# Edge sums in groups of six tiles instead of four, in a graph layer followed by a routed feed-forward layer

## The chip, the cores and the metric

The kernel runs on one core of a Trainium2 chip. A core has a matrix engine (PE, with its weight load PEld), a vector engine (DVE), a scalar engine (ACT), a general engine (POOL, GpSimd) and a queue engine (SP) that starts DMAs; POOL starts DMAs too, those with a list of row numbers among them. PE writes its products into PSUM, eight banks of 512 float32 numbers a partition; DVE and ACT read them there. The metric is the device time of one execution in microseconds, the median of several runs. All arithmetic is in float32.

## The reference, cut to what matters

```
N, E, H = 10000, 5000, 512
xn   = layernorm(x)                                  # each of the 10000 rows
msg  = relu(xn[src] + edge_attr @ W_e + b_e)         # 5000 edges x 512
aggr = segment_sum(msg, dst, N)                      # messages added into rows
h    = (1 + eps) * xn + aggr
h    = silu(batchnorm(h @ W1 + b1))                  # 512 -> 1024
x    = x + silu(batchnorm(h @ W2 + b2))              # 1024 -> 512
x    = x + ffn(layernorm(x))                         # routed, groups of 16 tokens
```

The edges are sorted by dst, and low rows are hit more often than high ones, so neighbouring edges often have the same target.

## The kernel before, in words

The work has stages: the edge sums, the first product with its statistics, the second product, and the feed-forward layer. The change touches the edge stage alone, the first 220 us or so. Line numbers are those of the kernel before.

**Tiles and groups.** The 5000 edges make 40 tiles of 128 (NTE), and the tiles make groups of EG = 4, ten groups. A DMA that adds rows into agg (in device memory) may not name a row twice, and two of them that run together may not touch the same row. So the kernel first adds up, within a group, all messages with the same target.

**Preparation.** SP fills agg with zeros (L212), in 11 DMAs, behind the loads of the edge data. POOL gathers the x rows of the first 20 tiles (L235). PE makes for each group a tile "row" that holds the group's targets along the free axis (`targets`, L245). DVE compares with it and counts, for each edge, earlier edges of its group with the same target (L256). An edge that is not the first gets a spare row behind the N real ones as its target (L261 to L264): to_i holds the row numbers. agg has AGG_ROWS = 83 x 128 rows for that.

**Messages.** For each group DVE makes the masks `same[i]` (L288): which edges of tile i have the target of which edges of tiles 0 to i. PE multiplies the edge attributes by W_e into a bank pm (L294), DVE adds the gathered row times its layer-norm scale (L295), ACT takes the relu (L296). Layer-norm statistics of the group after (`norm`, L273 to L277) come in between: DVE's statistics, ACT's square root (L275), DVE's reciprocal.

**Sums.** For tile i of a group PE adds into a bank pc the products of same[k][:, i] with the messages of tile k, for k from i to the end of the group (L304): 4 + 3 + 2 + 1 = 10 products a group. ACT copies the bank back into the tile (L306), and POOL starts the adding DMA (L307). The first sum of a group waits until all sums of the group before have landed (L311); those of one group run together, told apart by views of agg (L58). Behind the sums of a group POOL gathers the next four tiles, until all 40 are there. pm and pc have three banks each, and "row" two.

**What sets the order.** Each engine works off its own instructions in one order, which a planner writes from the program and from its own estimates; an instruction that waits holds up all that stand behind it. So instructions of other stages appear inside the edge stage: on DVE the 16 copies ctl (L492), that rearrange a small weight (the controller) of the last stage, on ACT and POOL the layer norm of the first rows of the next stage (L357 to L365). SP works in order too: after the zeros come small constants, two loads of x rows (L340), the controller (L73) and two small tables; then loads into buffers that were lent to the edge tiles: W2 (L327), x rows of the last stage (L560) and W1 (L395), each of which waits for the sums of those tiles to land.

**After the stage.** The next stage loads rows of agg (L346), which waits for all sums, adds them to the normalized rows (L376), turns them on PE (L379), and goes into a long run of products (L133).

Of the kernel before, what the change touches and what calls it, by code (L numbers as in the profile page):

```python
# [8 lines left out]
F32 = mybir.dt.float32  # L9
# [6 lines left out]
N, H, E, ED = 10000, 512, 5000, 64  # L16
# [6 lines left out]
P = 128  # L23
# [6 lines left out]
TE = P  # L30
NTE = -(-E // TE)
EP = TE * NTE
EG = 4
AGG_ROWS = 83 * P
assert AGG_ROWS > N + EG * TE
G = CH // T

# [13 lines left out]
def gnn_ffn_kernel(ctx: ExitStack, tc: tile.TileContext, a: dict, out: bass.AP):  # L51
    nc = tc.nc
    x = a["x"]


    agg = tc.dram_tile([AGG_ROWS, H], F32, name="agg")

    views = bass_types.dram_disjoint_views(agg, EG)  # L58

# [118 lines left out]
    with tc.tile_pool(name="pe1", bufs=1) as pe1, tc.tile_pool(name="pe", bufs=2) as pe, \  # L178
# [4 lines left out]
        def by_tile(name, past, dtype):  # L183
            flat = a[name][:whole * TE, :].rearrange("(t e) o -> t (e o)", e=TE)
            i = pe1.tile([NTE, TE], I32, name=name + "_i")
            nc.vector.memset(i, past)
            nc.sync.dma_start(out=i[:whole, :], in_=flat)
            nc.sync.dma_start(out=i[whole:NTE, :E - whole * TE], in_=a[name][whole * TE:E, :].rearrange("e o -> o e"))
            f = pe1.tile([NTE, TE], F32, name=name + "_r")
            nc.vector.tensor_copy(f, i)  # L190
            pt = ps_e.tile([TE, NTE], F32, name="row")
            nc.tensor.transpose(pt, f, ident[:NTE, :NTE])
            t = pe1.tile([TE, NTE], dtype, name=name + "_t")
            nc.vector.tensor_copy(t, pt)
            return t

        src_i = by_tile("src", 0, I32)
        dst_f = by_tile("dst", AGG_ROWS - 1, F32)
        eat = pe1.tile([ED + 1, EP], F32, name="eat")
# [9 lines left out]
        nc.sync.dma_start(out=eat[:ED, :E], in_=a["edge_attr_64"])  # L209
        for r0 in range(0, AGG_ROWS, 8 * P):  # L210
            j = min(8, (AGG_ROWS - r0) // P)
            nc.sync.dma_start(out=agg[r0:r0 + j * P, :].rearrange("(p j) d -> p j d", j=j),  # L212
                              in_=zero.to_broadcast([P, j, H]))


        before = pe1.tile([TE, EG, TE], F32, name="before")
        nc.gpsimd.memset(before, 1.0)
        nc.gpsimd.affine_select(out=before[:, EG - 1, :], in_=before[:, EG - 1, :], compare_op=ALU.is_gt, fill=0.0,
                                base=0, pattern=[[-1, TE]], channel_multiplier=1)
        groups = NTE // EG  # L220
        spare = pe1.tile([TE, groups, EG], F32, name="spare")
        nc.gpsimd.iota(spare, pattern=[[0, groups], [TE, EG]], base=N, channel_multiplier=1,
                       allow_small_or_imprecise_dtypes=True)
# [9 lines left out]
        def gather(t0, t1):  # L233
            for t in range(t0, t1):
                tc.keep_in_program_order(nc.gpsimd.indirect_dma_start(  # L235
                    out=xgs[t], out_offset=None, in_=x,
                    in_offset=bass.IndirectOffsetOnAxis(ap=src_i[:, t:t + 1], axis=0)))

        gather(0, NTE // 2)

        def targets(g):

            row = ps_e.tile([TE, EG, TE], F32, name="row")
            for i in range(EG):
                nc.tensor.transpose(row[:, i, :], dst_f[:, g * EG + i:g * EG + i + 1].to_broadcast([TE, TE]), ident)  # L245
            return row

# [2 lines left out]
        count = pe1.tile([TE, NTE], F32, name="count")  # L250
        for g in range(groups):
            row = targets(g)
            for i in range(EG):
                t = g * EG + i
                junk = pe.tile([TE, EG, TE], F32, name="junk", bufs=1)
                nc.vector.scalar_tensor_tensor(junk[:, :i + 1, :], row[:, :i + 1, :], dst_f[:, t:t + 1],  # L256
                                               before[:, EG - 1 - i:, :], op0=ALU.is_equal, op1=ALU.mult,
                                               accum_out=count[:, t:t + 1])
        away = pe1.tile([TE, NTE], F32, name="away")
        nc.vector.tensor_scalar(count, count, 1.0, None, op0=ALU.min)  # L260
        nc.vector.tensor_sub(away, spare.rearrange("p g i -> p (g i)"), dst_f)  # L261
        nc.vector.tensor_mul(away, away, count)
        to_i = pe1.tile([TE, NTE], I32, name="to_i")
        nc.vector.tensor_add(to_i, away, dst_f)  # L264

        def norm(g):

            st = pe.tile([TE, EG, 6], F32, name="st")
            mv = pe.tile([TE, EG, 2], F32, name="mv")
            rs = pe.tile([TE, EG, 1], F32, name="rs")  # L270
            sh = pe.tile([TE, EG, 1], F32, name="sh")
            for i in range(EG):
                tc.keep_in_program_order(nc.vector.bn_stats(out=st[:, i, :], in_=xgs[g * EG + i]))  # L273
                nc.vector.bn_aggr(out=mv[:, i, :], in_=st[:, i, :])
            nc.scalar.activation(rs, mv[:, :, 1:2], AF.Sqrt, bias=eps_t, scale=1.0)  # L275
            nc.vector.reciprocal(rs, rs)
            nc.vector.scalar_tensor_tensor(sh, mv[:, :, 0:1], -1.0, rs, op0=ALU.mult, op1=ALU.mult)  # L277
            return rs, sh

        last = []  # L280
        ln = norm(0)
        for g in range(groups):
            row = targets(g)

            same = [pe.tile([TE, i + 1, TE], F32, name=f"same{i}") for i in range(EG)]
            for i in range(EG):
                t = g * EG + i
                nc.vector.tensor_scalar(same[i], row[:, :i + 1, :], dst_f[:, t:t + 1], None, op0=ALU.is_equal)  # L288
            rs, sh = ln
            for i in range(EG):  # L290
                t = g * EG + i
                xg = xgs[t]
                pm = ps_e.tile([TE, H], F32, name="pm", bufs=3)
                nc.tensor.matmul(pm, lhsT=eat[:, t * TE:(t + 1) * TE], rhs=we, start=True, stop=True)  # L294
                tc.keep_in_program_order(nc.vector.scalar_tensor_tensor(xg, xg, rs[:, i, :], pm, op0=ALU.mult, op1=ALU.add))  # L295
                nc.scalar.activation(xg, xg, AF.Relu, bias=sh[:, i, :], scale=1.0)  # L296
            if g + 1 < groups:
                ln = norm(g + 1)
            sums = []
            for i in range(EG):  # L300
                t = g * EG + i
                pc = ps_e.tile([TE, H], F32, name="pc", bufs=3)
                for k in range(i, EG):
                    nc.tensor.matmul(pc, lhsT=same[k][:, i, :], rhs=xgs[g * EG + k], start=(k == i),  # L304
                                     stop=(k == EG - 1))
                nc.scalar.copy(xgs[t], pc)  # L306
                sums.append(tc.keep_in_program_order(nc.gpsimd.indirect_dma_start(  # L307
                    out=views[i], out_offset=bass.IndirectOffsetOnAxis(ap=to_i[:, t:t + 1], axis=0),
                    in_=xgs[t], in_offset=None, compute_op=ALU.add)))

            for done in last:  # L311
                tc.add_manual_dep(sums[0].ins, done.ins.name, mybir.DependencyInfo(
                    mybir.DependencyClass.Sync, mybir.DependencyReason.DATA), reason="sums in turn")
            last = sums
            at = NTE // 2 + g * EG
            gather(at, min(at + EG, NTE))
# [210 lines left out]
    pe, dve, act, pool = (InOrder(e) for e in (nc.tensor, nc.vector, nc.scalar, nc.gpsimd))  # L527
# [434 lines left out]
```

## Time and profile before

| what | value |
|---|---|
| median of three runs | 1968.99 us (1967.05 to 1970.73) |
| the profiled execution | 1968.09 us, span 1966.4 us |
| granted PE clock, mean over the span | 0.967 |
| first sum into agg issued | 79.47 us |
| last sum issued, end of issue | 213.86 us |
| first addition of agg rows (L376) | 222.34 us |
| POOL, one sum, issue to issue | 1.86 us |
| POOL, one gather, issue to issue | 1.25 to 1.3 us |
| DMA of a sum, issue to landing | 4.8 / 6.1 / 9.6 us (least, median, most) |
| ten products of a group (L304), at full clock | 8.75 us |

Times within the execution count from the start of the span. A row in order of time gives start, duration, engine, line, operation, output and inputs, shape, and how many were merged (x20: a float32 product of PE is recorded as two instructions), and in brackets the idle time of the engine before it with what ended it. A row of the waits gives the one that waited, what for, total us, how often, and the longest.

### The profile page before, as it was taken

The numbers are of one execution on the slowest core, as the hardware profiler recorded it, in microseconds if no ns is written. First come the engines' busy times: TensorE is split into PE (matmuls) and PEld (weight loads), VectorE is DVE, ScalarE is ACT, GpSimd is POOL, SyncE is SP. The second block draws the span as 40 slices with busy tenths as digits, with TensorE's granted clock in tenths as the row PEclk, the third lists the DMA queues.
The fourth block names the chain that finished last, engine by engine and source line by source line (L and its number), as shares of the span: only waits on it lengthen the run. The fifth ranks groups of instructions, "written<-read, shape, count | busy, mean of one in ns | idle before, by whom it ended". The sixth has DMA issues, their size and how long they took to land. (4 is left out here: it accounts for less than half of the span.)

```text
span 1966.4 us, 43924 instructions
## 1 busy us (share of the span) xinstructions
PE 1792.2 (91%) x19354; PEld 1029.4 (52%) x19354; DVE 1207.8 (61%) x1894; ACT 722.5 (37%) x973; POOL 621.5 (32%) x626
## 2 busy tenths in 40 slices
PE   5959399999999997999999999589999999999985
PEld 2424144444444443444444444367777777777763
DVE  8547276777777767434334334327787777777766
ACT  0324233333333315222222220255555555555432
POOL 4275333333233314333333331122323232323311
PEclk9979599999999998999999999699999999999998
DMA  9997444443444312333333331742232323232101
GB/s 349 301 228 143 99 169 170 162 158 151 162 162 162 140 42 84 125 147 128 143 125 126 125 126 42 237 129 88 87 112 79 120 79 120 80 119 70 45 24 57
DMA packets 95219, 256.37 MB, mean 130 GB/s; under 512 B 7845, under 2 KB 8435, under 8 KB 94452
## 3 DMA queue, kind: packets, MB, share of 16 engines
q1 hardware_dynamic: 86068, 232.58, 32.5%
q0 software_dynamic: 8960, 20.98, 5.3%
q8 instruction: 152, 2.49, 0.5%
q14 instruction: 39, 0.32, 0.0%
HBM read 143.47 MB, written 110.07 MB: 129 GB/s over the span
## 5 line engine op out<-in xcount | busy, mean ns | idle before, releaser
L133 PE MATMUL x<-h_s,w_u 128*128 128x500 f32 x640 | 289.1, 584 | 0.3 <-POOL h_s L123 0.3
L525 ACT COPY gs<-pb 128x1024 f32<-128x1024 f32 (+2 forms) x168 | 161.5, 1027 | 123.6 <-PE pb L525 112.0
L133 PEld LDWEIGHTS x<-h_s,w_u 128*128 128x128 f32 x640 | 122.4, 191 | 148.2 <-issue 142.9
L525 DVE STREAM_TRANSPOSE it<-it 128x1024 f32<-128x1024 f32 x152 | 174.9, 1209 | 0.1
L525 PE MATMUL pi<-gs,f_sb 128*64 128x64 f32 x5120 | 165.9, 225 | 3.3 <-ACT gs L525 1.7
L525 POOL TENSOR_TENSOR pv<-perm,odd_t 64x512 f32<-64x512 f32 (+1 forms) x80 | 99.8, 1248 | 206.8 <-PE pb L525 178.2
L525 PEld LDWEIGHTS pi<-gs,f_sb 128*64 128x64 f32 x5120 | 157.3, 140 | 11.0 <-issue 2.2
L525 PE MATMUL pb<-bd,xl 32*128 32x128 f32 x2504 | 144.7, 285 | 15.1 <-ACT it L525 8.8
L143 DVE SCALAR_TENSOR_TENSOR t<-w,s 128x500 f32<-128x500 f32 x60 | 40.7, 678 | 188.5 <-PE w L133 184.8
L133 PE MATMUL z<-h_s,w 128*128 128x500 f32 x320 | 148.3, 586 | 3.9 <-POOL h_s L123 3.9
L525 PE MATMUL pb<-f_sb,ib 32*32 32x256 f32 x5120 | 134.7, 385 | 14.2 <-ACT it L525 8.6
L525 DVE COPY it<-pb 128x1024 f32<-128x1024 f32 x76 | 93.1, 1225 | 88.6 <-PE pb L525 88.5
L133 PE MATMUL z<-h_s,w_u 128*128 128x500 f32 x320 | 144.0, 583 | 0.3 <-POOL h_s L123 0.3
L525 PEld LDWEIGHTS pb<-bd,xl 32*128 32x128 f32 x2504 | 129.0, 188 | 27.7 <-ACT it L525 13.6
L123 POOL TENSOR_TENSOR h_s<-hc 128x500 f32<-128x500 f32 x60 | 77.0, 1316 | 149.1 <-PE z L133 149.1
L525 ACT COPY it<-pb 128x1024 f32<-128x1024 f32 x76 | 79.0, 1039 | 112.1 <-PE pb L525 112.1
L138 ACT COPY s<-z 128x500 f32<-128x500 f32 x60 | 34.5, 575 | 220.2 <-PE z L133 156.4
L525 POOL TENSOR_SCALAR ln_rs<-ln_mv 128x4 f32<-128x4 f32 (+2 forms) x22 | 4.9, 224 | 302.5 <-DVE ln_mv L525 302.4
L525 PEld LDWEIGHTS pb<-f_sb,ib 32*32 32x32 f32 x5120 | 70.2, 103 | 57.1 <-ACT it L525 14.6
L133 PEld LDWEIGHTS z<-h_s,w_u 128*128 128x128 f32 x320 | 60.8, 190 | 73.9 <-issue 72.7
L123 POOL TENSOR_TENSOR h_s<-hb 128x1000 f32<-128x1000 f32 x30 | 69.6, 2335 | 91.5 <-PE z L133 65.3
L433 DVE BATCH_NORM_STATS2 st<-h 128x6 f32<-128x500 f32 x144 | 93.7, 671 | 1.3
(180 smaller groups left out, 3084.9 us busy)
## 6 DMA issues: line engine op xcount, KB each, us to landing
h1s<-h SPq DMA_DIRECT2D x36, 1000.0 KB
agg<-zero SPq DMA_DIRECT2D x10, 2048.0 KB
xt<-in_x_dram SPq DMA_DIRECT2D x20, 1000.0 KB
hc<-h1s SPq DMA_DIRECT2D x20, 1000.0 KB
h2s<-h SPq DMA_DIRECT2D x20, 1000.0 KB
x<-in_x_dram SPq DMA_DIRECT2D x39, 512.0 KB
out_dram<-x SPq DMA_DIRECT2D x39, 512.0 KB
yt<-h2s SPq DMA_DIRECT2D x76, 256.0 KB
```

Of the source, the lines that this page charges most:

```text
L123: eng.tensor_tensor(t[:, k0:k1], q(*x0, k0, k1), q(*x1, k0, k1), op)
L133: nc.tensor.matmul(bank, lhsT=us[n][:, k, m * P:(m + 1) * P], rhs=bs[n][k], start=start and k == 0, stop=k == kb - 1, skip_group_check=True)
L138: nc.scalar.copy(kept[n], banks[n])
L143: nc.vector.scalar_tensor_tensor(dst, banks[x0], sc, kept[x1], op0=op, op1=ALU.add)
L433: nc.vector.bn_stats(out=st1[:, 4 * r + m, 2 * i + t, :], in_=h1[:, r, t, :])
L525: return lambda *args, **kw: tc.keep_in_program_order(f(*args, **kw))
```

## The change

EG becomes 6: the 40 tiles make six groups of six and a last one of four. `tiles(g)` gives the number of tiles of a group. A group of six has 6 + 5 + 4 + 3 + 2 + 1 = 21 products pc. "row" takes a whole two banks for each of its two buffers (eight tiles wide), so pm and pc get two banks each, where they had three. AGG_ROWS grows to 85 x 128 for the spare rows of wider groups. The gathers behind a group's sums become six, until all 40 tiles are there.

```
-EG = 4
-AGG_ROWS = 83 * P
+EG = 6
+AGG_ROWS = 85 * P
...
-        groups = NTE // EG
+        groups = -(-NTE // EG)
...
+        def tiles(g):
+            return min(EG, NTE - g * EG)
...
-            row = ps_e.tile([TE, EG, TE], F32, name="row")
-            for i in range(EG):
+            row = ps_e.tile([TE, 8, TE], F32, name="row")
+            for i in range(tiles(g)):
                 nc.tensor.transpose(row[:, i, :], dst_f[:, g * EG + i:g * EG + i + 1].to_broadcast([TE, TE]), ident)
...
-            for i in range(EG):
+            for i in range(tiles(g)):
                 t = g * EG + i
                 xg = xgs[t]
-                pm = ps_e.tile([TE, H], F32, name="pm", bufs=3)
+                pm = ps_e.tile([TE, H], F32, name="pm")
...
-            for i in range(EG):
+            for i in range(tiles(g)):
                 t = g * EG + i
-                pc = ps_e.tile([TE, H], F32, name="pc", bufs=3)
-                for k in range(i, EG):
+                pc = ps_e.tile([TE, H], F32, name="pc")
+                for k in range(i, tiles(g)):
                     nc.tensor.matmul(pc, lhsT=same[k][:, i, :], rhs=xgs[g * EG + k], start=(k == i),
-                                     stop=(k == EG - 1))
+                                     stop=(k == tiles(g) - 1))
```

Without a `bufs` of its own a tile of this pool has two buffers. The other loops over a group's tiles (the counting, the statistics, the masks) change from EG to tiles(g) in the same way.

## The prediction

> **What bounds the kernel now.** I read the page first. PE is busy for 91% of the span, and of its digits (one for 49 us) the first, third and fifth are 5, 5 and 3; after them only the 26th and the last are as low. The change lies in those first five, so I asked for the waits up to 260 us, then for the instructions in order of time, engine by engine.
>
> ```profile
> PE 1792.2 (91%) x19354; PEld 1029.4 (52%) x19354; DVE 1207.8 (61%) x1894; ACT 722.5 (37%) x973; POOL 621.5 (32%) x626
> ...
> PE   5959399999999997999999999589999999999985
> ```
>
> ```profile
> POOL agg L307 <- DMA L_gnn_eps_sb<-in_L_gnn_eps_dram: 49.4, 1, 49.4
> DVE xt L376 <- DMA at<-agg: 31.7, 7, 23.7
> ...
> DVE ctl L492 <- DMA L_ffn_controller_sb<-in_L_ffn_controller_dram: 26.0, 1, 26.0
> ```
>
> Three waits matter. The first sum into agg waits until 79.5 us for the zeroing. The next stage waits for the last sum (L376). In between DVE stands 26 us at a copy that has nothing to do with the edges. Which engine paces the sums? POOL in order of time, from the eighth group on:
>
> ```profile
> 175.34 1.55 POOL L307 DMA_INDIRECT agg<-xg,to_i  x1 [5.12 <-ACT xg L296]
> ...
> 180.92 1.55 POOL L307 DMA_INDIRECT agg<-xg,to_i  x1 [0.31 <-issue]
> 189.90 1.55 POOL L307 DMA_INDIRECT agg<-xg,to_i  x1 [7.43 <-ACT xg L306]
> ...
> 202.74 1.61 POOL L307 DMA_INDIRECT agg<-xg,to_i  x1 [2.82 <-DMA agg<-xg,to_i]
> ...
> 207.63 1.64 POOL L307 DMA_INDIRECT agg<-xg,to_i  x1 [0.86 <-ACT xg L306]
> ...
> 212.31 1.55 POOL L307 DMA_INDIRECT agg<-xg,to_i  x1 [0.30 <-issue]
> ```
>
> An issue costs 1.86 us, and each group then waits about 5.2 us for the landing of the one before (ACT, named here, had made its last copy for the group of 175.34 by 170.1). The train runs from 79.47 to 213.86. Now PE and the stalled DVE and ACT:
>
> ```profile
> 85.00 8.75 PE L304 MATMUL pc<-xg,same 128*128 128x512 f32 x20
> ...
> 119.33 2.08 PE L294 MATMUL pm<-we,eat 65*128 65x512 f32 x2 [22.14 <-DVE xg L295]
> 121.20 11.33 PE L304 MATMUL pc<-xg,same 128*128 128x512 f32 x20
> 132.37 3.60 PE L294 MATMUL pm<-we,eat 65*128 65x512 f32 x8
> 135.81 8.75 PE L304 MATMUL pc<-w,same 128*128 128x512 f32 x20
> ...
> 157.29 3.60 PE L294 MATMUL pm<-we,eat 65*128 65x512 f32 x8
> ...
> 182.21 3.60 PE L294 MATMUL pm<-we,eat 65*128 65x512 f32 x8
> 185.65 8.75 PE L304 MATMUL pc<-xg,same 128*128 128x512 f32 x20
> ```
>
> ```profile
> 115.27 0.30 ACT L275 ACTIVATE rs<-mv,eps_t 128x4 f32<-128x4 f32 x1 [26.06 <-DVE mv L274]
> 115.48 1.54 ACT L306 COPY xg<-pc 128x512 f32<-128x512 f32 x3
> ```
>
> After its stall PE runs without a gap: 132.37, 157.29 and 182.21 are two groups apart each, 12.46 us a group. That is 14 products of 0.858 us (8.58 us from 135.81 to the next work, ten products) and four transposes (0.44). So two trains of 12.5 us a group run side by side, and PE ends 19.5 us ahead of POOL (194.4 against 213.9): the sums end last today, and PE is just under them. The stall hides: by 97 us PE has finished four groups, and POOL issues the fourth at 125.2.
>
> **The change, part by part.** The sum is made on the profiled execution: 1968.09 us, span 1966.4; the median of the three runs is 0.9 us above it.
>
> Products. A group of n tiles has n(n+1)/2 products pc. Before: 10 x 10 = 100. After: 6 x 21 + 10 = 136. The 36 more cost 36 x 0.858 = 30.9 us of PE. A group of six is 21 + 6 products and six transposes: 27 x 0.858 + 0.66 = 23.8 us, 3.97 a tile; before it was 3.12. The sums by themselves would take 6 x 1.86 + 5.2 = 16.4 us a group. PE becomes the pace.
>
> Start. The counting at L256 gets tiles up to 768 wide. Pitches in the trace are 0.39, 0.53, 0.66, 0.79 (128 to 512); continued by 0.13 they make 4.4 us a group of six, 29.0 in all against 24.5. Also ahead of the first message: four more masks (L288; pitches .27 to .66 seen, .79 and .92 continued: 3.5 us) and two more statistics (0.7 each). DVE starts the first message at 51.9 instead of 43.9. PE then has 25 products, 21.5 us, and 2.9 us for its low clock (the 11.33 above against 8.75, and the slow pm): first group done near 77. Its last copy is still ahead of the zeroing's end. That end moves by the 256 more rows: 0.52 MB at 410 GB/s, 1.3 us, to 80.8. So both are covered, with 3 us to spare; past that they count one for one. Fewer square roots and reciprocals (7 groups, not 10) and POOL's wider memset before the gathers (POOL idles 2.7 us there) cost nothing.
>
> The stall. This decides. In the instruction order of the changed kernel, DVE meets the ctl copies (L492) inside the statistics of the third group, when 12 tiles are done, not 16. ACT takes square root L275 of that group after the first copy of the second group. With two banks for pc, the second group's pc 0 and 1 fill both, pc 2 takes the bank of pc 0, and pc 3 needs ACT's copy of pc 1, which stands behind that square root. So PE stops near 94 us with six products of the second group undone (3 + 2 + 1), and POOL, having issued one sum of that group near 100, waits at the second. Before, three banks and a later place left only copies undone (115.48).
>
> When does the controller land? The x loads stand before it in SP's ring: 2 x 1.02 MB. The DMA view gives packets, MB and share of that ring (q1), first for 80 to 84 us, then for 84 to 96:
>
> ```profile
> q1 hardware_dynamic: 221, 0.45, 30.7%
> ...
> q1 hardware_dynamic: 290, 0.58, 14.0%
> ```
>
> Alone it moved 113 GB/s; beside POOL's sums and gathers 48. After, all starts 1.3 us later, and POOL's ring is busy to about 104 us (six sums, six gathers, one sum), so 0.45 MB by 85.3 and 18.7 us x 48 GB/s make 1.35 MB; the 0.70 MB left take 6.2 us at 113 GB/s; with 1.3 us for the controller's rest and its landing (my allowance) that is 111.5, against 114.9. Ends: 98 (POOL's ring costs nothing) and 118.
>
> The Trainium skill ("DMA: Bandwidth & Descriptors", section "SWDGE vs HWDGE vs iDMA") says an engine takes turns between the two kinds of queue. With equal turns alone the x loads would keep a half, 56 GB/s, and the controller would land about 1.4 us earlier. The row shows less than half, and I go by the row.
>
> From 111.5 on: DVE copies and last statistics 1.6, square root and one copy 1.0: PE resumes at 114.1. Six products at low clock: today PE resumes at 119.3 and is granted full speed near 126.4, so some four products at 1.72 and two at 0.86, 8.4 us: second group done at 122.5. Masks for the next group wait for the last product (1 us), under the pm of that group. Then four groups of six: 4 x 23.8 = 95.2. For gaps I take 2.5: in the fifth group the transposes come first, six masks (3.6 us) and then the messages, and two pm banks don't cover that (about 1.8). Bounds: 0 (no PE gap at all today) and 8 (2 a group). Sixth group done: 220.2.
>
> Its last sums: the copies of the last three come within 2.6 us, an issue is 1.86, so the last issue ends 3.5 us after PE; landing 5.2: 228.9. Longest issue-to-landing of a sum today is 9.6 us, so +4 is the other end. Then the four of the last group, held by the layer norm of the next stage on POOL and ACT: today 202.74 to 213.86, 11.1; in the new order two of those POOL operations (0.87 and 1.05) come after the first sum, not in its wait, and again before the third: 14.2. End: 243.1, 29.2 us after 213.86. The weights and rows that SP loads into lent buffers (L327, L395, L560) also come later. The nearest to the path is L395: issued 174.8 today with 18 us to its first use; after, near 205 (the fifth group done at 196 and its landing), so 223, and 5.7 us of weight sums on DVE: covered by 14 us, one for one past that. From the last landing on the order of every queue is as before, and the wait at L376 passes all of it on. 1968.1 + 29.2 = 1997.3; on the median's level 1998.
>
> What the change gains, three landings fewer of 5.2 us, 15.6 us, falls where POOL now waits for PE. The Trainium skill (same page, "Anatomy of one DMA — SWDGE (gpsimd) path") gives a fixed cost of about 2.0 us a DMA; by it the gain would be 6 us at best, and the forecast wouldn't move.
>
> **The rivals.**
> - *The stall is short* (the controller lands before DVE asks). Then PE runs on from 77: five groups 119 + 2.5 = 198.6, then 8.7 and 14.2: 221.5, 7.6 us later: 1976. For it: most of its packets may be through near 98. Against: today's 114.9.
> - *Faster: the sums stay the pace.* Three groups with gathers (11.2 + 7.6, landing to 20): 59; three of 16.5; tail 14.2: 80.8 + 122.7 = 203.5, 10.4 us earlier: 1958. It decides if a group of six costs PE under 22.4 us with no stall, or far less with one. Against: 0.858 recurs in every group.
> - *No change*: it needs the stall gone and the tail as short as today's.
> - *Worse*: stall to 118, gaps of 8, slow landings and six sums that don't overlap (the data of the four from 150.5 on take 9.5 us in the DMA records; of six, 14, still under PE's 23.8): 1998 + 6.5 + 5.5 + 4 = 2014 and more.
>
> **How the numbers follow.** Forecast 0.64 (1984 to 2014), short stall 0.15, faster 0.07, no change 0.03, worse 0.11. The range from 1976 to 2014 leaves out the last three. A measurement tells 0.2%, about 4 us. Faster 0.07, same 0.03, slower 0.90.
>
> **What would show it.** PE pitch of 24 us a group of six; a hole in PE from the mid-nineties to about 114; ACT's square root ending it; the second sum of the second group after 114; POOL waiting for ACT's copies, not for landings, from then; last sum near 243. Wrong if ctl is copied near 100, if the pitch is under 22, or if POOL's last wait is shorter.

## The result and the profile after

The changed kernel takes 1999.93 us (median of 6 runs, 1994.65 to 2005.69), against 1966.22 us before on the same chip: a ratio of 1.0167, 95% interval 1.0145 to 1.0190. It is slower, by 33.7 us; the forecast was 1998.0 us. The profiled execution took 2000.55 us, span 1998.8 us.

The page's busy line and PE's digits (one for 50 us) of the kernel after:

```profile
PE 1826.1 (91%) x19426; PEld 1040.5 (52%) x19426; DVE 1215.7 (61%) x1888; ACT 722.9 (36%) x970; POOL 623.8 (31%) x626
...
PE   3969679999999998999999999589999999999986
```

PE is busy 33.9 us longer, 30.9 us of that being the 36 products more. The digits that have changed are the first, third, fifth and sixth, and, by one, the 16th and the last. PE after, in order of time:

```profile
79.29 1.88 PE L297 MATMUL pm<-we,eat 65*128 65x512 f32 x4
...
115.43 7.81 PE L307 MATMUL pc<-x,same 128*128 128x512 f32 x12 [17.63 <-ACT w L309]
123.08 1.88 PE L297 MATMUL pm<-we,eat 65*128 65x512 f32 x4
...
146.58 1.88 PE L297 MATMUL pm<-we,eat 65*128 65x512 f32 x4
...
219.90 2.99 PE L297 MATMUL pm<-we,eat 65*128 65x512 f32 x6
...
238.51 2.08 PE L307 MATMUL pc<-xg,same 128*128 128x512 f32 x2 [6.89 <-ACT xg L309]
255.19 1.06 PE L382 MATMUL pt<-ident,xt 125*128 125x125 f32 x4 [14.60 <-issue]
```

The first row behind a group's products marks that group's end: 79.29, 123.08, 146.58, 170.01, 196.46, 219.90 (the fourth, a row of transposes, and the fifth are not shown). PE stands from 97.8 to 115.43 with six products of the second group undone, and after that it is the pace, 23.5 us a group. The next stage begins at 255.19 instead of 223.14, 32.05 us later, and from there both kernels need the same (1743.6 and 1743.3 us to the end of the span). POOL after, with what ended its waits:

```profile
100.32 1.62 POOL L310 DMA_INDIRECT agg<-w,to_i  x1 [0.88 <-DMA agg<-w,to_i]
115.66 1.57 POOL L310 DMA_INDIRECT agg<-w,to_i  x1 [13.72 <-ACT w L309]
...
184.65 1.62 POOL L310 DMA_INDIRECT agg<-w,to_i  x1 [8.19 <-ACT w L309]
...
228.93 1.55 POOL L310 DMA_INDIRECT agg<-xg,to_i  x1 [5.22 <-DMA agg<-xg,to_i]
...
232.06 2.12 POOL L362 TENSOR_SCALAR ln_rs<-ln_rs,L_gnn_eps_sb 125x4 f32<-125x4 f32 x1
...
238.75 1.64 POOL L310 DMA_INDIRECT agg<-xg,to_i  x1 [2.31 <-ACT xg L309]
...
244.82 1.61 POOL L310 DMA_INDIRECT agg<-xg,to_i  x1 [0.18 <-issue]
```

POOL, which before waited about 5 us for the landings of most groups, now waits for bank copies, that is, for PE. From 228.93 on the last four sums take 17.5 us, where four back to back take 7.1 (three steps of 1.86 and 1.55). What ended PE's stop stands in the rows of DVE and of ACT:

```profile
113.11 0.25 DVE L495 COPY ctl<-L_ffn_controller_sb 128x16 f32<-128x16 f32 x2 [22.76 <-DMA L_ffn_controller_sb<-in_L_ffn_controller_dram]
```

```profile
114.61 0.30 ACT L278 ACTIVATE rs<-mv,eps_t 128x6 f32<-128x6 f32 x1 [23.91 <-DVE mv L277]
```

DVE stands at the copy of the controller, ACT at the square root behind DVE's statistics, PE at a bank that ACT has not copied, POOL at a sum whose tile is not copied: one late load of 128 KB stops four engines.

### The profile page after: what moved, and what is told of

It is laid out like the page before. It is cut to its first block, busy times and chain, and to the rows that moved or that the text cites. A ratio compares the mean times of both kernels' runs of the same rounds, so it can differ in the third digit from the quotient of the medians.

```text
span 1998.8 us, 44066 instructions
## 1 busy us (share of the span) xinstructions
PE 1826.1 (91%) x19426; PEld 1040.5 (52%) x19426; DVE 1215.7 (61%) x1888; ACT 722.9 (36%) x970; POOL 623.8 (31%) x626
## 4 chain that ended last, share of the span: by engine, by line
PE 69%; DVE 9%; DMA 7%; ACT 5%; POOL 4%; SPq 3%; issue 2%; POOLq 0%; ACTq 0%; DVEq 0%
PE pb L528 17%; PE pi L528 10%; PE x L133 9%; PE z L133 9%; PE v L133 5%; PE w L133 5%; PE pc L307 4%; PE y L133 3%; PE ps L528 3%; SPq L212 3%; DVE ln_st L357 2%; ACT xt L368 2%; ACT it L528 2%; PE pt L133 2%; DMA L_ffn_controller_sb<-in_L_ffn_controller_dram 2%
## 5 line engine op out<-in xcount | busy, mean ns | idle before, releaser
L528 PEld LDWEIGHTS pi<-gs,f_sb 128*64 128x64 f32 x5120 | 155.9, 139 | 12.6 <-issue 3.7
```

The source lines that it names most:

```text
L528: return lambda *args, **kw: tc.keep_in_program_order(f(*args, **kw))
```

## The experiments

All are compared with the kernel before on the same chip. Line numbers in the edits are those of the kernel after, or of before where the kernel is made from it.

| kernel | median us | ratio to before (95%) | next stage begins |
|---|---|---|---|
| before | 1966 to 1969 | 1 | 223.14 |
| after | 1999.93 | 1.0167 (1.0145 to 1.0190) | 255.19 |
| a_late | 1978.93 | 1.0053 (1.0037 to 1.0069) | 235.94 |
| a_few | 1990.91 | 1.0116 (1.0097 to 1.0134) | 245.87 |
| a_few_late | 1957.20 | 0.9938 (0.9918 to 0.9958) | 211.72 |
| b_late | 1967.51 | 0.9991 (0.9976 to 1.0006) | 222.03 |
| b_two_banks | 1974.71 | 1.0026 (1.0010 to 1.0043) | 226.28 |
| a_ring | 2009.88 | 1.0234 (1.0193 to 1.0274) | 267.58 |
| b_late_tail | 1978.90 | 1.0064 (1.0041 to 1.0087) | 232.58 |
| five_late_tail | 2003.85 | 1.0183 (1.0157 to 1.0210) | 254.76 |
| b_late_end | 1965.86 | 0.9989 (0.9976 to 1.0002) | 217.96 |
| a_late_end | 1969.59 | 1.0010 (0.9992 to 1.0028) | 224.01 |
| five_late_end | 1956.58 | 0.9935 (0.9916 to 0.9954) | 210.61 |

The last column is from one profiled execution of each, in us of its span; from that point to the end they need 1742 to 1750 us.

**The stop alone: a_late.** After, with the 16 copies of the controller and one reduction that needs another late table kept behind the weight sums of the second product in DVE's order. No other engine's order changes.

```
-                nc.vector.tensor_copy(
+                tc.keep_in_program_order(nc.vector.tensor_copy(
...
-    nc.vector.tensor_reduce(odd_p, ...)
+    tc.keep_in_program_order(nc.vector.tensor_reduce(odd_p, ...))
```

> The changed kernel, with the 16 ctl copies and the small sum behind them (L495, L505) kept in DVE's order until after the weight sums of the second product; nothing else moves in the edge stage. Stall theory: PE's hole of 17.6 us (97.8 to 115.4) goes, and with it the wait of POOL at the second sum of the second group. PE then runs groups of 23.5, 23.5, 23.4, 26.4 and 23.4 us from 79.3 on, the sixth group is done near 199.5 instead of 219.9, and the end comes 20 us earlier, less 1.8 us for the copies that now stand at the start of the last stage: about 1981, a ratio to the kernel before of 1.008. Rival, six sums in flight land slowly and set the pace: no gain, 1998 to 2000. Rival, PE's products aren't the pace: the gain is larger, to 1965 or less.

A hit: 1978.93 us, 1.0053. PE runs on with group ends at 100.75, 124.25, 147.69, 177.28 and 200.72, still 23.5 us apart (29.6 once, where PE stood 1.45 us ahead of the fifth group and two of its products, at 152.88, took 3.62 us instead of 1.88). So the stop was about 20 us of the 33.7: the medians differ by 21.0 us, the two profiled executions by 17.3, and the next stage begins 19.3 us earlier. The pace of PE together with the end of the train are the rest.

**Fewer products: a_few.** After, with three products for each tile of a group of six at most, 15 instead of 21; sums between tiles three or more apart are left out.

```
-                for k in range(i, tiles(g)):
+                ks = range(i, min(i + 3, tiles(g)) if tiles(g) == EG else tiles(g))
+                for k in ks:
```

> The changed kernel, with the products of a group of six cut from 21 to 15: for tile i only k = i to i+2 (sums between tiles three or more apart in a group are left out). All 100 products, as many as before; six sums in flight, two banks and the stall stay. Theory of PE's pace: 18.7 us a group of six after the stall, not 23.8; the stall ends near 113 as in the changed kernel, six products are then undone as there, sixth group done near 201, last issue near 228 instead of 246: about 1981. Rival, the landings or POOL set the pace after the stall: no more than 4 us gained.

A miss by 10 us, and the most useful one: the stop grew. The row of DVE in a_few:

```profile
124.27 1.25 DVE L496 COPY ctl<-L_ffn_controller_sb 128x16 f32<-128x16 f32 x15 [35.80 <-DMA L_ffn_controller_sb<-in_L_ffn_controller_dram]
```

The same load was copied at 124.27 instead of 113.11, though DVE asked for it 1.9 us sooner. With fewer products PE had the second group done before it stopped, so its six sums all went out by about 111. The DMA queues between 104 and 112 us (packets, MB, share of 16 engines; q0 is POOL's, q1 SP's), after first, a_few next:

```profile
q1 hardware_dynamic: 798, 0.77, 28.4%
q0 software_dynamic: 153, 0.31, 17.7%
```

```profile
q0 software_dynamic: 557, 1.03, 88.9%
q1 hardware_dynamic: 259, 0.39, 14.9%
```

With POOL's queue at 89% SP's queue moved half as much. The other kernels after it whose stop is gone or elsewhere agree: in a_late, a_few_late, a_late_end and a_ring SP's queue moved 0.38 to 0.47 MB in the same 8 us, with POOL's queue at 86 to 91%. The stop is thus coupled to POOL's transfers, the sums and the gathers behind them: what sends them out sooner makes the controller later. This is the term that the forecast took from the trace of before, and the two kernels show it side by side. The forecast's two rates, 48 GB/s beside POOL's transfers and 113 alone, are less clean than it has them: in the window of the 113 POOL's queue had 42.7% of the engines' time.

**Both: a_few_late.**

> Both edits: 15 products a group of six (those between tiles three or more apart are left out) and the ctl copies late. Theory: with PE and the stall out of the way POOL's train is the pace: 80.9, three groups of 19.4 with gathers, three of 16.5, then 11 to 17 us for the last four sums: the last issue ends between 200 and 206, 8 to 14 us ahead of the kernel before, which makes 1954 to 1962 (1.8 us for the late copies counted). That is the gain of three landings fewer, which PE covers in the changed kernel. Rival, six in flight land so much later that three landings fewer bring nothing: 1966 or more.

A hit: 1957.2 us, 0.9938. With a group at 18 to 19 us of PE and no stop, the landings pace the train, first sums from 81.03 by some 19.4 us and then 16.0 to 17.7, and three landings fewer do pay. That is the forecast's rival "the sums stay the pace", priced at 1958. It was the right price for a kernel in which PE costs 19 us a group or less.

**The same copies late in before: b_late.**

> The kernel before with the ctl copies late. Theory: its stall of 26 us on DVE is hidden, since POOL issues the fourth group's sums after it ends; PE then runs ahead of POOL without the hole, POOL's train stays: 1964 to 1970, the same within 0.2%. Rival, the stall costs the kernel before too: 10 us or more gained.

A hit: no difference (1967.51 us). PE finished at 168.7 us and the train did not move. Before had the same wait of 26 us on DVE; its train covered it.

**The banks alone: b_two_banks.**

```
-                pm = ps_e.tile([TE, H], F32, name="pm", bufs=3)
+                pm = ps_e.tile([TE, H], F32, name="pm")
...
-                pc = ps_e.tile([TE, H], F32, name="pc", bufs=3)
+                pc = ps_e.tile([TE, H], F32, name="pc")
```

> The kernel before with two banks instead of three for pm and for pc, nothing else. Theory (the banks have little part in the loss: TensorE was done with the weight sums at 168.7 us while the last sum was issued near 203 us, so some 19 us of slower products are hidden): 1964 to 1971 us, the train of sums within 1 us of before. Rival (the banks are a cause by themselves): 5 us or more above before, with the first sums of the groups later than 19.3 us after one another.

Between the two: 1.0026, about 5 us (2 to 8.5), and not where the rival looked for it. The new banks also made the planner change POOL's order: all five layer-norm operations now stand between the first and the second sum of the last group, as in after, where before has two of them ahead of the first. Up to the last group the train is not later; its first sum goes out at 201.15, 1.6 us earlier than in the profile of before. Then the last product waits for a bank. PE in b_two_banks:

```profile
209.05 2.08 PE L304 MATMUL pc<-xg,same 128*128 128x512 f32 x2 [8.74 <-ACT xg L306]
```

The copy that frees the bank stands on ACT behind two scales of the next stage (207.01), and these behind layer-norm operations on POOL. The last issue ends at 216.97 instead of 213.86. The last group's four sums take 15.8 us, where before needs 11.1. So the loss of b_two_banks is at the very end of the train, and no other place shows in the train. How much of it is the banks and how much the other order on POOL, this run doesn't separate.

**The controller first in SP's queue: a_ring.** After, with the load of the controller moved ahead of the two loads of x rows.

```
+        ctl_in = load_const("L0_ffn_controller", ...)
         ep1 = load_const("L0_gnn_eps", ...)
...
-    ctl_in = load_const("L0_ffn_controller", ...)
```

> The kernel after with the load of the controller's gates moved ahead of the x loads in SyncE's queue, so that it lands before the sums begin. Theory (TensorE's stop of 17.6 us is VectorE's wait for this load, behind which the messages of the third group stand; it lands late because SyncE's queue moves slowly beside the sums): the load lands before 86 us, the stop falls to under 5 us, 1978 to 1984 us, as with the copies put later in VectorE's order. The reduction that needs the gate masks, two loads further on in the same queue, stays where the planner puts it; if it becomes the next wait, TensorE stops there by 5 to 15 us and the time lies at 1985 to 1995 us. Rival (the copies wait for something else than the load's place): 1996 to 2003 us.

The theory's own half came true and the time was outside all that it allowed: 2009.88 us. The copies ran at 83.58 without a wait. DVE then met the reduction of the gate masks, in the third group's statistics (a_ring, DVE):

```profile
127.30 0.16 DVE L505 TENSOR_REDUCE odd_p<-c_gmask_sb 128x2 f32<-128x8 f32 x1 [36.47 <-DMA c_gmask_sb<-in_c_gmask_dram]
```

PE stood 27.3 us. I had allowed 5 to 15. SP's rows show why; those of after first, then those of a_ring (start, duration on SP's queue):

```profile
79.88 1.26 SPq L343 DMA_DIRECT2D xt<-in_x_dram  x2
81.18 20.70 SPq L73 DMA_DIRECT2D L_ffn_controller_sb<-in_L_ffn_controller_dram  x1
```

```profile
80.38 1.28 SPq L344 DMA_DIRECT2D xt<-in_x_dram  x2
81.71 25.61 SPq L501 DMA_DIRECT2D tie<-in_c_tie_dram  x2
107.36 1.95 SPq L73 DMA_DIRECT2D c_gmask_sb<-in_c_gmask_dram  x1
```

Whatever stands behind the 2 MB of x rows takes their time, 21 us or 26. In both kernels the planner had put the readers of these tables among the messages. And as no stop held up the second group's sums, SP's queue was slowed for longer, as in a_few.

**The end of the train, first try: b_late_tail, and groups of five with it: five_late_tail.** The code of the layer-norm statistics moved ahead of the last group's sums, with marks that keep its order on POOL and ACT.

```
+            if g + 1 == groups:
+                for t in range(2):
+                    blks[t].load_x(t)
+                    blks[t].stats(tc.keep_in_program_order)
             sums = []
```

> The kernel before with the controller's copies late in VectorE's order and the end of the train put in order: the layer-norm statistics of the next stage stand ahead of the last group's messages on VectorE and POOL, and the last group's bank copies ahead of the scales on ScalarE, so that its sums go out back to back. Theory: the last issue ends about 4 us earlier than in before (211.7 us there): 1962 to 1965 us. Rival (the layer norm merely moves in front of the train and delays it, or the next stage waits for the rows anyway): within 2 us of before, or slower.

> Groups of five (115 + 5 = 120 products of tiles for 8 groups, seven landings between groups instead of nine in before and six in after), three banks as in before, the controller's copies late and the end of the train in order as in the run beside this one. Theory (with the stop gone and TensorE's group of five near 18.5 us, below the 19.4 us that one group of sums and its landing take, the train gets its gain from two landings fewer): last issue ends near 204 us, 1956 to 1962 us, below both kernels. Rival (TensorE paces the groups of five too, 8 groups of 19 us and over from 79 us): last issue after 212 us, 1966 to 1975 us.

Both missed, mainly for a reason that has nothing to do with the end of the train. (The end of before is 213.86; the 211.7 in the first expectation is the start of b_late's last issue.) With the code of the constants moved ahead of the groups, DVE meets a constant that waits for a load behind the zeroing, ahead of the first messages. DVE in b_late_tail:

```profile
79.63 0.15 DVE L287 TENSOR_SCALAR L_gnn_eps_sb<-L_gnn_eps_sb 128x1 f32<-128x1 f32 x1 [34.75 <-DMA L_gnn_eps_sb<-in_L_gnn_eps_dram]
```

The first sum then goes out at 92.96 (98.57 with five) instead of 79.5. The last four sums of b_late_tail did go back to back, 215.65 to 222.88, and its train of 129.9 us is 4.5 us shorter than the one of before. But the rival of the first expectation shows too: the layer norm, moved in front of the last sums, holds them up. In b_late_tail its ten operations stand on POOL from 206.83 to 215.08, and the wait between the last two groups is some 4 us longer than in before. In five_late_tail POOL waited 9.63 us there for DVE's statistics; from the seventh group's first sum to the eighth's took 30.0 us, where five_late_end, below, needs 13.7. That costs it 16.3 us, about as much as the late start (18.5), and TensorE's pace costs the groups before it 10.5.

**The end again, by marks alone: b_late_end, a_late_end, five_late_end.** Nothing moves in the code. Marks keep the last group's bank copies ahead of the scales on ACT, and the layer norm's ten operations behind the last sum on POOL.

```
-                nc.scalar.copy(xgs[t], pc)
+                (tc.keep_in_program_order if g + 1 == groups else lambda i: i)(nc.scalar.copy(xgs[t], pc))
...
+                keep(nc.gpsimd.tensor_scalar(rs[:RT], mv[:RT, :, 1:2], EPS, None, op0=ALU.add))
...
+            blks[t].stats(tc.keep_in_program_order)
```

> The kernel before with the controller's copies late, and the end of the train in its program order by marks alone, with no code moved: the last group's four bank copies ahead of the eight scales on ScalarE, and the layer norm's ten operations behind the last sum on POOL. Theory (the last three sums are held by bank copies that stand behind scales, which wait for layer-norm operations on POOL): the four sums go back to back from 202.1 us, the last issue ends near 209.5 instead of 213.2 us; the layer norm now comes behind them and takes 3 to 7 us beside the landing of the sums, so up to all of the 3.7 us can be lost again: 1963.5 to 1967.5 us. Rival (the rows of the next stage wait for the layer norm, not for the sums): 1969 us and over.

Within the expected range: 1965.86 us, 0.9989. The last issue ends at 208.31, 5.0 us earlier than in b_late, and the next stage begins 4.1 us earlier, but the interval (0.9976 to 1.0002) still holds no change. The layer norm that now comes last costs little: its five operations take 2.4 us (208.39 to 210.80).

> The kernel after with the controller's copies late and the end of the train in program order by the same marks. Theory (with two banks the fourth product of the last group waits for a copy that stands behind the scales, so more is held here than before the change): six sums back to back from 209.6 us, last issue end 220.4 instead of 227.3 us, 1971 to 1976 us; what then remains over before is TensorE's pace of 23.4 us a group. Rival (the tail is set by the landing of the fifth group's sums or by the products): 1978 to 1981 us, as without the marks.

The theory, and by more than I had counted: 1969.59 us, 1.0010 (0.9992 to 1.0028). My 220.4 was a miscount, since the last group has four sums and not six; 209.6 and four sums make 216.7. The last issue ended at 215.0, 12.2 us earlier than in a_late, 2.7 of that because the last group's first sum was earlier. Groups of six without the stop and without the held end are as fast as before, no faster: the three landings fewer go to PE's pace.

> Groups of five, three banks, the controller's copies late and the end in program order by marks. From the spoiled run of groups of five: TensorE's pitch is 17.4 us a group (19.4 once), first sums 107.2 us from the first to the seventh group, so 80.1 + 107.2 + 17.5 = 204.8 us for the last group's first sum, and 10.7 us for its five sums: last issue end 215.5 us, against 213.9 us in before. Theory (groups of five are paced by TensorE from 79 us on, so they give back what two landings fewer save): 1964 to 1972 us, no gain worth the name. Rival (the landings pace the groups of five, each landing fewer is worth 5 us): 1956 to 1962 us.

Here the rival holds: 1956.58 us, 0.9935, faster than both kernels. TensorE's pitch is 17.4 us a group in both runs of groups of five; what was different in the spoiled run, five_late_tail, was PE's start, at 86 us, 12.6 us ahead of its first sum. In this one PE starts at 48 us, 32 us ahead, stays ahead, and the landings pace the train, POOL in five_late_end:

```profile
80.09 1.63 POOL L310 DMA_INDIRECT agg<-w,to_i  x1 [50.34 <-DMA L_gnn_beta_sb<-in_L_gnn_beta_dram]
...
190.48 1.55 POOL L310 DMA_INDIRECT agg<-xg,to_i  x1 [4.76 <-DMA agg<-xg,to_i]
...
199.72 1.56 POOL L310 DMA_INDIRECT agg<-xg,to_i  x1 [0.30 <-issue]
```

The wait ahead of the last group (4.76) is one for a landing again, as before the change, but there are seven and not nine, and the last issue ends at 201.28, 12.6 us ahead of before. It is the version to keep. Contrary to both expectations, groups of five had two banks for pm and pc, as in after, and not three: the edit is made from after and leaves the banks. With the same marks, groups of four take 1965.86 us (three banks), of five 1956.58 and of six 1969.59 (two banks each), so five are worth 9.3 us against four, with 7.0 us at the last issue. How much groups of five give without the two kinds of marks, or with three banks, was not tried.

## Why the prediction was right, step by step

It said slower, 1998.0 us in 1976 to 2014; 1999.93 was measured. The steps, with forecast and measurement in us of the span:

| step | forecast | measured |
|---|---|---|
| first group's products done | 77 | 79.3 |
| first sum (end of the zeroing) | 80.8 | 80.90 |
| PE stops | near 94 | 97.8 |
| controller there | 111.5 | 113.1 |
| PE resumes | 114.1 | 115.43 |
| six products at low clock | 8.4 | 7.65 |
| second group done | 122.5 | 123.08 |
| four groups, gaps included | 97.7 | 96.8 |
| sixth group done | 220.2 | 219.90 |
| first sum of the last group | 228.9 | 228.93 |
| last issue ends | 243.1 | 246.43 |

*Products.* The pitch was 23.5, 23.4, 26.45 and 23.4 us a group of six, against 23.8. The gap of the fifth group is where it was forecast, 3 us and not 1.8: masks and messages there come behind the transposes, and two pm banks don't cover them.

*Start.* The low side: 79.3, not 77, and the last copy at 80.07. The forecast's own terms make 53.3 us for the first message where it writes 51.9 (43.9 + 4.5 + 3.5 + 1.4); 52.50 was measured. The products at low clock cost about 4.3 us instead of 2.9. Of the 3 us of cover 0.8 was left. It held, so it cost nothing.

*The stall.* Place and chain are right: DVE's copy, ACT's square root, the third pc bank, POOL at the second sum of the second group. a_late shows its price, about 20 us. The controller landed 1.6 us later than forecast. Up to 104 us SP's queue had moved 1.40 MB, against 1.35 forecast; then it moved at 96 GB/s (the 0.77 MB in 8 us above) and not at the 113 of the sum, which makes some 1.1 of the 1.6 us. That the rate falls beside POOL's transfers a_few shows by a second case.

The granted clock, in slices of 1 us, goes down at 103.2 in after, 5.4 us after PE stopped, and is full again at 120.3, 4.9 us after it resumed; in before it goes down 1.9 us after the stop (97.2) and is back 7.1 us after PE resumes (119.3). So three of the six products ran at half clock (3 x 1.72 + 3 x 0.86 = 7.7; 7.65 measured, where the forecast has 8.4 for four and two, which make 8.6). The Trainium skill ("TensorE: Matmul & The Clock Gate", section "What's actually happening") gives about 3.4 us of sustained work for the return, counted in a window that runs free. An estimate by it is two slow products, 6.9 us. Both returns here took longer, and the two differ by 2.2 us.

*The end.* This is the step that failed in size: "14.2" for the sums of the last group, where 17.5 was measured. The forecast had counted two of the layer norm's operations after the first sum (0.87 and 1.05). All five came there, and took 5.9 us from 230.56 to 236.44, and the last product waited 6.89 us for a bank. Their number alone doesn't make them dear. In a_few_late the same five stand at the same place and take 2.4 us (190.84 to 193.25), and the last four sums take 14.0 us, near the forecast's 14.2. What differs is what DVE does meanwhile. L101 is the first five additions of the weight sums of the next stage. In after they run beside POOL's operations. All engines of after, in order of time:

```profile
230.56 0.25 POOL L360 TENSOR_SCALAR ln_rs<-ln_mv 125x4 f32<-125x4 f32 x1
...
231.75 5.73 DVE L101 TENSOR_TENSOR w_u<-w 128x1024 f32<-128x1024 f32 x5
232.06 2.12 POOL L362 TENSOR_SCALAR ln_rs<-ln_rs,L_gnn_eps_sb 125x4 f32<-125x4 f32 x1
234.26 1.01 POOL L363 TENSOR_TENSOR ln_sh<-ln_mv,ln_rs 125x4 f32<-125x4 f32 x1
235.37 1.07 POOL L364 TENSOR_SCALAR ln_sh<-ln_sh 125x4 f32<-125x4 f32 x1
```

In a_few_late they are over before the last group (DVE, then POOL):

```profile
179.56 5.75 DVE L101 TENSOR_TENSOR w_u<-w 128x1024 f32<-128x1024 f32 x5
```

```profile
192.34 0.30 POOL L363 TENSOR_SCALAR ln_rs<-ln_rs,L_gnn_eps_sb 125x4 f32<-125x4 f32 x1
192.73 0.20 POOL L364 TENSOR_TENSOR ln_sh<-ln_mv,ln_rs 125x4 f32<-125x4 f32 x1
193.02 0.23 POOL L365 TENSOR_SCALAR ln_sh<-ln_sh 125x4 f32<-125x4 f32 x1
```

The forecast had these weight sums as 5.7 us of DVE "covered by 14 us". On DVE they were covered; on POOL, beside them, its operations took 3.5 us longer. That is the term that was mis-sized; the other 7 us or so over four sums back to back, from the order on POOL and ACT and the two banks, the forecast had. All profiles agree with it (last section), but no run moves the weight sums alone. a_late_end takes the whole hold away and is worth 9.3 us.

*Where the loss went, then.* By the medians: the stop 21.0 us (1999.9 to 1978.9), the held end 9.3 (1978.9 to 1969.6), and 1.7 are left against before, which the interval of a_late_end (-1.6 to +5.5 us) doesn't tell from nothing. In before the held end is there too, worth some 4 us at the start of the next stage by b_late_end. The change's own gain, three landings fewer, was used up by PE, as forecast: a_late and a_few_late differ in the products alone, by 21.7 us.

*The rivals.* "The stall is short" was priced at 1976, with the last issue at 221.5; a_late is that kernel, took 1978.9 and had it at 227.25. Of these 5.7 us 3.5 are the end of the train that was mis-sized, and the rest is the late start. "Faster" was priced at 1958, and a_few_late, where PE doesn't pace, took 1957.2. So both were near as prices, and the condition decided, a group of six at 23.5 us of PE.

*Luck.* Some of the agreement is errors that cancel. The last group's first sum came within 0.03 us because PE resumed 1.3 us late while the six products and the four groups took 0.75 and 0.9 us less than forecast and the last sums and their landing 0.3 more. The total is 1.9 us off although the loss was 33.7 us where the forecast's sum has 29.2, since before took 1966.22 us beside this run and not the 1968.99 that the forecast added to.

## What to carry to other kernels

When steps are grouped to save waits between them, work out what the group costs the engine that runs beside: the work here grows with the square of the group, and the best of the three sizes run, five, is the one that still stays under the train. Look for every instruction on an in-order engine that waits for a late load of another stage: it costs nothing as long as a longer chain runs beside it (before), and about 20 us as soon as a bank behind it runs out (after); keeping it late in the order cost nothing that b_late shows (0.9991). Move code that the planner orders with care: three of these runs lost time because a constant's reader came to stand ahead of messages. And count what a neighbouring engine does beside a short chain of small operations: here it made the chain twice as long.

## What the runs showed that was not expected

A load on SP's queue gets slower the more POOL's transfers, sums and gathers, are in flight: 0.77 MB in 8 us beside POOL's queue at 18%, 0.39 MB beside 89%. Quicker products therefore made the stop longer, 35.8 us instead of 22.8 on DVE. The Trainium skill says that an engine goes round robin between the two kinds of queue ("DMA: Bandwidth & Descriptors", section "SWDGE vs HWDGE vs iDMA"); from that the forecast had worked out equal turns, and at 14.9% against 88.9% of the engines' time the turns were not equal by time here.

The small layer-norm operations on POOL (125x4) take 0.2 to 0.3 us, the power 1.05, and the issue of a sum 1.55 to 1.66. In after three of them took some five to seven times as long (2.12, 1.01, 1.07 where 0.30, 0.20, 0.23 are the least). In all thirteen profiles the slow rows of the edge stage stand beside DVE's five additions L101 (128x1024, 5.7 us): the same three operations in a_late, a_few and a_ring (2.30 to 2.45, 1.01, 1.07 or 1.08), operations of 0.99 to 1.87 us in b_late_tail and five_late_tail, and every issue of a sum that took over 1.7 us (1.91 to 2.41, in seven profiles). The exceptions are four operations of 0.86 or 0.87 us in before and b_late, which start while the issue of a sum still runs. In five_late_tail five operations take 2.4 us just ahead of the additions (226.06 to 228.47), and the same five 5.9 us beside them (229.22 to 235.15), with no DMA moving from 229 to 234.7. In b_late_tail the operations are back at 0.23 us from 212.42 on, just after the additions end (212.27). In a_few_late, b_late_end and five_late_end the layer norm runs clear of the additions and is quick. A sum issued just before is thus not what makes them slow. That the additions are the cause is an inference from rows that fall together; why they would slow POOL stays open.
